# Perceiver block on one core: the last keys' probabilities copied to both partition halves, their values computed 512 queries wide amid the next scores, and the left key's scalings pinned in order

## The chip, the cores and the metric

The kernel runs on one core of one Trainium2 chip. The metric is device time in microseconds. A core has TensorE (PE) for matmuls, VectorE (DVE), ScalarE (ACT) and GpSimd (POOL) for the rest, and SyncE (SP), whose queue issues most of the transfers here; ACT's queue issues a few too. Each engine runs its own list of instructions in order and waits on semaphores for the others.

## The reference

Six sublayers follow each other, each added to `x` (8 batches of 64 tokens, width 512): cross attention, a block attention with a Fourier transform, a mixture of experts, a second cross attention, an attention with relative positions and a ternary feed-forward. The change touches the first sublayer alone:

```python
x = x + _L0_xattn_ref(_layernorm(x, axis=-1), ctx_1024, mask_BxS2_bf1,
                      L0_xattn_Wq, L0_xattn_Wkv, L0_xattn_Wout, L0_xattn_b_out)
```

It has 16 heads of width 64. For each batch and head the 64 queries are scored against 1601 keys that come from `ctx_1024` (8 x 1601 x 512), a softmax over the masked scores follows, the probabilities weigh the values, and a projection returns to width 512. All of it is float32.

## The kernel before

**Tiling.** The function `l0_xattn` holds this sublayer. The key weights are folded into the queries, so that scores are `ctx` times a 512-wide query (`qk`) and values are a 512-wide mixture of `ctx` rows (`a`), which the value weights turn afterwards (`v_ps`, line 699). A step takes one batch and half of the heads: 512 columns (4 head pairs g, 2 heads h of each, 64 queries q), so there are 16 steps. Even steps begin a new batch.

**Keys.** The 1601 keys are 12 blocks of 128 (`LAST`), 64 more (the *tail*), and one single *left* key. The 12 blocks are taken as 6 pairs. For each pair the product is formed with seven smaller products instead of eight (a Strassen-like scheme, class `Run`): `mul(..., n, ...)` is product n, and `p1`, `p5`, `u2`, `c11`, `c12`, `c22`, `c21` are its partial results and sums. Products 7 and 4 of one pair are issued within the next pair (`seventh`, `fourth`). In the scores, ACT copies `p1`, `p5` and `u2` out of PSUM and makes `c21`; DVE makes `c11`, `c12` and `c22`, and the running maximum `m` (lines 481, 484). Products 6, 7 and 4 add into the same PSUM tile `x_`, so 7 comes after `u2` has been copied from it and 4 after `c22` has read it. The four extra operands per key pair are made by `Quarters.left` on POOL, lines 138 to 141, 24 operations for a batch. In odd steps the finished key columns are read back from memory (`kept`), with no POOL work.

**Tail.** Its scores lie in `tail`: 256 columns, head h of each pair on partition half h. `attend_tail` (line 630) multiplies these probabilities with the tail's `ctx` rows, which lie on both halves: eight matmuls of 64 rows by 256 columns (line 641), whose results ACT copies into `a` (line 645). `attend` then adds the 12 blocks' values onto `a`.

**Left key.** Its score is a weighted sum over the 512 rows of `qk`: ACT scales the four row blocks (lines 492 and 497, tiles `by` and `by_c` of one tag with two buffers), POOL adds three times (line 498), and two matmuls against ones (`one_ps`, line 516) sum over partitions.

**Order.** A step of the loop at line 735 records: loads, `scores` of this step, `attend_tail` of the step before, `top_of` (transposes `m` with `m_ps`, reduces it and spreads it again with `top_ps`), `attend` of the step before, and `softmax` of this step. The text is not the order on the engines. A list scheduler, which works with modelled durations, orders each engine's instructions; `tc.keep_in_program_order` pins an instruction behind the one recorded last on its engine. Before the change only the writes to `kept` (line 205) are pinned in this stage.

**PSUM.** `ps_x`, `ps_y` and `ps_z` have two banks each for the products; `ps_m` has two for everything else (tag `mm`): tail scores, `one_ps`, `a_ps`, `m_ps`, `top_ps`, sums and side work. Side work of other parts (queries of the other batches, ternary weights) runs between, through `some` and `aside`.

Of the kernel before, what the change touches and what calls it, by code (L numbers as in the profile page):

```python
# [10 lines left out]
F32 = mybir.dt.float32  # L11
# [3 lines left out]
AF = mybir.ActivationFunctionType  # L15
# [5 lines left out]
P = 128  # L21
B, S, D = 8, 64, 512
NT = B * S // P
DC = D // P
# [3 lines left out]
NG = 8  # L28
# [87 lines left out]
H2 = P // 2  # L116
NK = len(KT)
TAIL, LAST = KT[-1][1], NK - 1
HALF = NG // 2 * P
QH = HALF // 2  # L120
NPAIR = LAST // 2
WIDE = LAST * HALF + 2 * QH
assert TAIL == H2 + 1


# [18 lines left out]
def l0_xattn(K, x, d, ternary, kept):  # L144
# [6 lines left out]
    tc, nc = K.tc, K.nc  # L151
    with ExitStack() as es:
# [19 lines left out]
        zp = es.enter_context(tc.tile_pool(name="a_z", bufs=1))  # L172

        def parts_of(wide):
            at = LAST * HALF
            return wide[:, :at].rearrange("p (k n) -> p k n", n=HALF), wide[:, ds(at, QH)], wide[:, at + QH :]

        def of_heads(t, h):
            return t.rearrange("p (g h q) -> p g h q", h=2, q=S)[:, :, h, :]
# [142 lines left out]
        norm_rest = K.normalizer(zp, x[:, 1:, :])  # L322
        load_weights(1)
        m8 = wp.tile([B * NK, P], U8, tag="m8", name="m8")
        m32 = tp.tile([P, QH], F32, tag="p1", name="m32")[: B * NK].rearrange("r (j n) -> r j n", j=2)
        nc.scalar.dma_start(m8, d["mask"])
        load_columns_tail(0)
        ctxT = load_columns(0)
# [76 lines left out]
        class Run:  # L405
# [6 lines left out]
            def add(self, mul, take):  # L412

                x_, y_, z_ = (
                    pool.tile([P, HALF], F32, tag=tag, name=f"{tag}_ps")[:, :QH]
                    for pool, tag in ((ps_x, "x"), (ps_y, "y"), (ps_z, "z"))
                )
                p1 = tp.tile([P, QH], F32, tag="p1", name="p1")
                u2 = tp.tile([P, QH], F32, tag="u2", name="u2")
                p5 = tp.tile([P, QH], F32, tag="p5", name="p5")  # L420
                mul(x_, 1, True)
                take.p1(p1, x_)
                self.seventh()
                mul(z_, 5, True)
                take.p5(p5, z_)
                mul(y_, 2, True)
                take.c11(y_, p1)
                self.fourth()
                mul(x_, 6, False)
                take.u2(u2, x_)  # L430
                mul(z_, 3, False)
                take.c12(z_, u2)
                self.before = mul, take, x_, p5
# [49 lines left out]
                    for k in (self.k, self.k + 1):  # L483
                        nc.vector.tensor_max(self.m, self.m, self.s[:, k, :])  # L484

        def scores(b, qkt, ctxT):
            qk, qt = qkt
            first = before is None
            wide = sp.tile([P, WIDE], F32, tag="s", name="s")
            s, tail, one = parts_of(wide)  # L490
            by = tp.tile([P, HALF], F32, tag="by", name="by")
            nc.scalar.activation(
                by, qk[:, 0, :], AF.Identity, bias=bias_left[:, b : b + 1], scale=left[:, 0, b : b + 1]
            )
            for c in range(1, DC):
                more = tp.tile([P, HALF], F32, tag="by", name="by_c")
                nc.scalar.activation(more, qk[:, c, :], AF.Copy, scale=left[:, c, b : b + 1])
                nc.gpsimd.tensor_add(by, by, more)
            m = tp.tile([P, HALF], F32, tag="m", name="m", bufs=1)
            right = {  # L500
                1: qk[:, 0:2, :QH], 2: qk[:, 2:4, :QH], 3: qk[:, 2:4, QH:],
                4: qt[:, 3], 5: qt[:, 0], 6: qt[:, 1], 7: qt[:, 2],
            }
            ps = ps_m.tile([P, HALF], F32, tag="mm", name="s_ps")[:, :QH]
            for c in range(DC):
                for h in range(2):
                    nc.tensor.matmul(
                        ps[ds(h * H2, H2)], lhsT=ctxT_tail[:, c, :], rhs=of_heads(qk[:, c, :], h),
                        start=c == 0, stop=c == DC - 1,
                    )  # L510
            nc.scalar.activation(tail, ps, AF.Identity, bias=bias_tail[:, b : b + 1], scale=1.0)

            def score_of_one():
                ps = ps_m.tile([P, HALF], F32, tag="mm", name="one_ps")[:, :QH]
                for h in range(2):
                    nc.tensor.matmul(ps[ds(h * H2, H2)], lhsT=ones, rhs=of_heads(by, h), start=True, stop=True)
                nc.scalar.copy(one, ps)

            if not first:
                score_of_one()  # L520
            run = Run()
            for i in range(NPAIR):

                def mul(ps, n, start, i=i):
                    for e in range(2):
                        nc.tensor.matmul(  # L526
                            ps,
                            lhsT=ctxT[i][:, Quarters.LEFT[n], ts(e, P)],
                            rhs=right[n][:, e, :],
                            start=start and e == 0,  # L530
                            stop=e == 1,
                            skip_group_check=not start,
                        )

                run.add(mul, Scores(s, m, b, i))
                some(2)
                next(aside, None)
                if first and i == NPAIR - 2:
                    score_of_one()
                if i == NPAIR - 1:  # L540
                    for h in range(2):
                        r = ds(h * H2, H2)
                        for rest in (tail, one):
                            m_h = of_heads(m[r], h)
                            nc.vector.tensor_max(m_h, m_h, rest[r].rearrange("p (g q) -> p g q", q=S))
            run.end()
            return wide, m

# [12 lines left out]
        def softmax(wide, top):  # L561

            parts = []
            s, tail, one = parts_of(wide)
            rest = wide[:, LAST * HALF :]
            for h in range(2):
                r = ds(h * H2, H2)
                rest_h = rest[r].rearrange("p (i g q) -> p i g q", i=2, q=S)
                nc.vector.tensor_sub(
                    rest_h, rest_h, of_heads(top[r], h).unsqueeze(1).to_broadcast([H2, 2, NG // 2, S])  # L570
                )
            nc.scalar.activation(rest, rest, AF.Exp)
            for k in range(0, LAST, 2):
                n = 2
                nc.vector.tensor_sub(s[:, k : k + n], s[:, k : k + n], top.unsqueeze(1).to_broadcast([P, n, HALF]))  # L575
# [14 lines left out]
            for h in range(2):  # L590
                r = ds(h * H2, H2)
                total_h = of_heads(total[r], h)
                nc.vector.tensor_add(total_h, total_h, tail[r].rearrange("p (g q) -> p g q", q=S))
            return parts, total, one

        class Mixed:
# [30 lines left out]
            def c21(self, ps):  # L627
                nc.vector.tensor_add(self.of(1, 0), ps, self.of(1, 0))

        def attend_tail(wide):  # L630

            a = tp.tile([P, DC, HALF], F32, tag="a", name="a", bufs=1)
            _, tail, _ = parts_of(wide)
            for c in range(0, DC, 2):
                heads = [
                    ps_m.tile([P, HALF], F32, tag="mm", name="a_ps").rearrange("p (i n) -> p i n", i=2) for _ in range(2)
                ]
                for i in range(2):
                    for h in range(2):
                        r = ds(h * H2, H2)  # L640
                        nc.tensor.matmul(
                            heads[h][:, i], lhsT=ctx_tail[r, ts(c + i, P)], rhs=tail[r], start=True, stop=True
                        )
                for h in range(2):
                    nc.scalar.copy(
                        a[:, c : c + 2].rearrange("p i (g h q) -> p i g h q", h=2, q=S)[:, :, :, h, :],
                        heads[h].rearrange("p i (g q) -> p i g q", q=S),
                    )
            return a

        def attend(b, half, soft, ctx, a, o, first):

# [31 lines left out]
            one = one.rearrange("p (g q) -> p g q", q=S)  # L684
            nc.vector.tensor_add(rs, sums, one)
            nc.vector.reciprocal(rs, rs)
            if b == 0:
# [47 lines left out]
        for step in range(2 * B + 1):  # L735
            if step < 2 * B:
                b, half = divmod(step, 2)
                if step:
                    now, ctxT = queries_of(b, half), load_columns(b, half)
                    if half == 0:  # L740
                        load_columns_tail(b)
                wide, m = scores(b, now, ctxT)
            if before:
                b0, half0 = divmod(step - 1, 2)
                a = attend_tail(before[0])
                if half0 and b0 + 1 < B:
                    load_rows_tail(b0 + 1)
            if step < 2 * B:
                top = top_of(m)
                if step == 1:  # L750
# [1757 lines left out]
```

## Time and profile before

| | us |
|---|---|
| median of three runs | 3070.31 (3068.79 to 3075.41) |
| profiled execution, its own time | 3067.53 |
| span of the profiled execution | 3065.8 |

The page gives busy times by engine, a picture of the span in 40 slices, the transfers, the chain of work that ended last, and the costliest groups. A group line names the kernel's line, engine and operation, out<-in, count, then busy us, mean ns, and the idle time before with what ended it. Some of the stage that the change touches:

```profile
L526 PE MATMUL x_ps<-qt,ctxT 128*128 128x256 f32 x1152 | 287.1, 383 | 12.6 <-DVE s L465 12.6
L665 PE MATMUL x_ps<-pt,ctx 128*128 128x256 f32 x1152 | 275.1, 381 | 0.6 <-DVE u L607 0.5
L138 POOL TENSOR_TENSOR ctx<-ctx 128x256 f32<-128x256 f32 x96 | 73.9, 770 | 605.9 <-DMA ctx<-in_ctx 461.3
```

Lines 526 and 665 are the products of the scores and of the values. Each float32 matmul leaves two records, so a product of the scores with its two matmuls shows as x4. Records of PE overlap their successors, so their durations add up to more than the time PE spends. The first sublayer takes about the first 1,525 us; the mean granted TensorE clock is 0.986.

A timeline line has the start and the duration of a run of equal instructions, engine, line and tiles, the count, and in brackets the idle time before it with what ended it. A line of the chain has start, duration, and what the time was spent in.

### The profile page before, as it was taken

Reading aid. Unit: us, or ns where it says so; the run is one execution under the profiler, and the core shown is the slowest. Engines: PE = TensorE matmul, PEld = TensorE weight load, DVE = VectorE, ACT = ScalarE, POOL = GpSimd, SP = SyncE. Lnnn points to the kernel's source line nnn. Section 1 sums busy time; section 2 is a strip of 40 time slices with the busy share of each in tenths; the row PEclk is TensorE's granted clock in tenths of the full one; section 3 lists DMA queues with packets and bytes.
Section 4 is the critical chain, followed back from the end, with each engine's and each line's share of the span. In section 5 each row is a group of like instructions: output and inputs, shape, how many; then the busy total and the mean of one; then the engine's idle time right before and its main releaser. Section 6 shows DMA issues by size and latency. Waiting matters only on the chain.

```text
span 3065.8 us, 41049 instructions
## 1 busy us (share of the span) xinstructions
PE 2965.6 (97%) x15650; PEld 2261.9 (74%) x15650; DVE 1917.8 (63%) x3383; ACT 878.3 (29%) x1636; POOL 924.6 (30%) x813
## 2 busy tenths in 40 slices
PE   8899999999999999999999999999999999999897
PEld 6777677787878887888745445788888888888764
DVE  4856455666667777666553243387677676676838
ACT  2422322233222232222021222333333323323224
POOL 3441342543625353442201001403404314224011
PEclk9999999999999999999999999999999999999989
DMA  9264364353655455352468986212021020120260
GB/s 320 79 223 160 115 219 173 118 190 136 219 194 190 165 180 187 107 191 101 162 216 313 345 283 203 73 33 77 5 89 52 28 89 29 51 91 10 101 86 14
DMA packets 288529, 430.52 MB, mean 140 GB/s; under 512 B 51126, under 2 KB 187326, under 8 KB 284110
## 3 DMA queue, kind: packets, MB, share of 16 engines
q1 hardware_dynamic: 273145, 389.59, 38.3%
q10 hardware_dynamic: 14549, 36.21, 3.3%
q8 instruction: 124, 2.03, 0.3%
q0 software_dynamic: 640, 2.10, 0.2%
q14 instruction: 71, 0.58, 0.1%
HBM read 352.80 MB, written 75.04 MB: 140 GB/s over the span
## 4 chain that ended last, share of the span: by engine, by line
PE 85%; DVE 6%; DMA 4%; POOL 2%; ACT 2%; issue 1%; SPq 0%; POOLq 0%; DVEq 0%; ACTq 0%
PE x_ps L1606 11%; PE x_ps L526 10%; PE x_ps L665 10%; PE y_ps L1606 8%; PE s_ps L1776 6%; PE z_ps L526 5%; PE z_ps L665 5%; PE oe_ps L1321 4%; PE h_ps L1294 4%; PE acc L1831 3%; PE y_ps L526 3%; PE y_ps L665 2%; DMA qk<-qk_all 2%; PE v_ps L699 1%; PE sum_ps L1653 1%
## 5 line engine op out<-in xcount | busy, mean ns | idle before, releaser
L1666 POOL TENSOR_TENSOR r<-r,minus_half 128x52 f32<-128x52 f32 x32 | 277.0, 8674 | 552.7 <-DVE r L1665 552.7
L526 PE MATMUL x_ps<-qt,ctxT 128*128 128x256 f32 x1152 | 287.1, 383 | 12.6 <-DVE s L465 12.6
L665 PE MATMUL x_ps<-pt,ctx 128*128 128x256 f32 x1152 | 275.1, 381 | 0.6 <-DVE u L607 0.5
L526 PEld LDWEIGHTS x_ps<-qt,ctxT 128*128 128x128 f32 x1152 | 216.5, 190 | 55.8 <-DVE s L465 20.8
L138 POOL TENSOR_TENSOR ctx<-ctx 128x256 f32<-128x256 f32 x96 | 73.9, 770 | 605.9 <-DMA ctx<-in_ctx 461.3
L665 PEld LDWEIGHTS x_ps<-pt,ctx 128*128 128x128 f32 x1152 | 216.9, 190 | 34.0 <-DVE a L622 1.6
L1776 PE MATMUL s_ps<-qb,kT 128*128 128x256 f32 x832 | 201.2, 382 | 0.0
L484 DVE TENSOR_TENSOR m<-m,s 128x512 f32<-128x512 f32 x160 | 131.0, 819 | 78.3 <-ACT s L479 76.2
L1776 PEld LDWEIGHTS s_ps<-qb,kT 128*128 128x128 f32 x832 | 155.0, 190 | 27.2 <-issue 4.9
L1786 DVE TENSOR_TENSOR s<-s_ps,r 128x512 f32<-128x512 f32 x192 | 126.7, 683 | 13.5 <-PE s_ps L1776 11.3
L465 DVE SCALAR_TENSOR_TENSOR s<-y_ps,bias,p 128x256 f32<-128x256 f32 x96 | 46.4, 483 | 131.7 <-PE y_ps L526 127.9
L1816 DVE TENSOR_TENSOR s<-s,top_ps 128x1792 f32<-128x1792 f32 x64 | 117.9, 1884 | 16.5 <-PE top_ps L1812 16.3
L1817 ACT ACTIVATE s<-s 128x1792 f32<-128x1792 f32 x64 | 101.1, 1591 | 66.2 <-DVE s L1816 66.2
L1831 PE MATMUL acc<-s,v 128*64 128x128 f32 x1664 | 115.9, 281 | 3.7 <-ACT s L1817 3.7
L1831 PEld LDWEIGHTS acc<-s,v 128*64 128x64 f32 x1664 | 98.4, 139 | 26.9 <-issue 22.6
L1294 PE MATMUL h_ps<-w,tok 128*128 128x512 f32 x256 | 117.3, 593 | 0.0
L575 DVE TENSOR_TENSOR s<-s,top_ps 128x1024 f32<-128x1024 f32 x96 | 115.9, 1210 | 0.4
L1321 PE MATMUL oe_ps<-w,hT 128*128 128x512 f32 x256 | 115.6, 593 | 0.0
L589 DVE TENSOR_TENSOR total<-total,s 128x512 f32<-128x512 f32 x160 | 112.5, 703 | 4.4 <-ACT s L576 0.9
L1313 ACT ACTIVATE hT<-hT_ps,L0f_be,L0f_g 128x128 f32<-128x128 f32 x128 | 55.5, 456 | 179.7 <-PE hT_ps L1312 116.9
L526 PE MATMUL x_ps<-qk,ctxT 128*128 128x256 f32 x384 | 103.8, 390 | 1.0 <-ACT s L479 1.0
L1606 PE MATMUL y_ps<-ctxT,L1x_WkT 128*128 128x256 f32 x384 | 102.2, 381 | 0.0
(476 smaller groups left out, 6351.3 us busy)
## 6 DMA issues: line engine op xcount, KB each, us to landing
w<-in_L0f_W SPq DMA_DIRECT2D x64, 1024.0 KB, 7.1
ctx<-in_ctx SPq DMA_DIRECT2D x192, 256.0 KB, 3.9
kept<-ctxT SPq DMA_DIRECT2D x48, 896.0 KB, 8.0
ctxT<-kept SPq DMA_DIRECT2D x48, 896.0 KB, 4.7
ctxT<-kept SPq DMA_DIRECT2D x24, 1792.0 KB, 7.2
ctxT<-in_ctxT SPq DMA_DIRECT2D x96, 256.0 KB, 4.4
wvT<-in_L0x_WvT SPq DMA_DIRECT2D x16, 1024.0 KB, 9.1
qk<-qk_all SPq DMA_DIRECT2D x15, 1024.0 KB, 6.4
```

Source lines behind the costliest of these rows:

```text
L484: nc.vector.tensor_max(self.m, self.m, self.s[:, k, :])
L526: nc.tensor.matmul(ps, lhsT=ctxT[i][:, Quarters.LEFT[n], ts(e, P)], rhs=right[n][:, e, :], start=start and e == 0, stop=e == 1, skip_group ...
L575: nc.vector.tensor_sub(s[:, k : k + n], s[:, k : k + n], top.unsqueeze(1).to_broadcast([P, n, HALF]))
L665: nc.tensor.matmul(ps, lhsT=ctx[pair][:, Quarters.LEFT[n], ts(m, P)], rhs=right[n][:, i, :], start=start and i == 0, stop=i == 2, skip_gro ...
L1294: nc.tensor.matmul(ps, lhsT=self.tok[:, c, :], rhs=self.w1[n][:, c, :], start=c == 0, stop=c == DC - 1)
L1321: nc.tensor.matmul(ps, lhsT=self.hT[:, f, :], rhs=self.w2[f // 4][:, f % 4, :], start=f == 0, stop=f == 15)
L1606: nc.tensor.matmul(ps, lhsT=left(n, e), rhs=right(n, e), start=start and e == 0, stop=e == 1, skip_group_check=not start,)
L1666: nc.gpsimd.tensor_tensor(r, r, minus_half, ALU.pow)
L1776: nc.tensor.matmul(ps[:, i].rearrange("p h q -> p (h q)"), lhsT=kT[c][:, ts(k0 + i, P)], rhs=qb[c].rearrange("p h q -> p (h q)"), start=Tr ...
L1786: nc.vector.tensor_mul(out, ps, by)
L1816: nc.vector.tensor_sub(part, part, top.to_broadcast([P, n, 2 * P]))
L1831: nc.tensor.matmul(acc[ds(64 * j, 64), c, :], lhsT=v[:, k, ds(c * P + 64 * j, 64)], rhs=s[:, k, ts(j, P)], start=k == 0, stop=k == NK - 1,)
```

## The change

The diff makes four edits to `l0_xattn`.

1. The tail's probabilities get a 512-wide place, like a key block. Each half computes its own heads' columns as before. After the exponential, two transfers on ACT's queue copy each half's columns to the other half, so that both halves hold all 512. They are pinned.
2. `attend_tail` is called for one pair of row blocks at a time, with two matmuls of 64 rows by 512 columns, one on each half, and two copies of 512 columns. The calls (`within`) stand within the next step's scores, after its third and fifth pair, no longer after the scores.
3. The maxima with `tail` and `one` stand at the third pair in all steps but the first, no longer at the last. The subtraction of the maximum and the exponential on `tail` and `one` are split into four and three instructions instead of two and one.
4. The left key's scalings on ACT and additions on POOL are pinned in program order, in all steps but the first. `p1` and `u2` keep one buffer each instead of two, as the wider place takes 1 KB more per partition in each of two buffers.

```diff
-WIDE = LAST * HALF + 2 * QH
+WIDE = (LAST + 1) * HALF + QH
...
-                p1 = tp.tile([P, QH], F32, tag="p1", name="p1")
-                u2 = tp.tile([P, QH], F32, tag="u2", name="u2")
+                p1 = tp.tile([P, QH], F32, tag="p1", name="p1", bufs=1)
+                u2 = tp.tile([P, QH], F32, tag="u2", name="u2", bufs=1)
...
-            nc.scalar.activation(
+            pinned = tc.keep_in_program_order if before else lambda ins: ins
+            pinned(nc.scalar.activation(
                 by, qk[:, 0, :], AF.Identity, bias=bias_left[:, b : b + 1], scale=left[:, 0, b : b + 1]
-            )
+            ))
...
-                nc.scalar.activation(more, qk[:, c, :], AF.Copy, scale=left[:, c, b : b + 1])
-                nc.gpsimd.tensor_add(by, by, more)
+                pinned(nc.scalar.activation(more, qk[:, c, :], AF.Copy, scale=left[:, c, b : b + 1]))
+                pinned(nc.gpsimd.tensor_add(by, by, more))
...
-                if i == NPAIR - 1:
+                if i == (NPAIR - 1 if first else 2):
                     for h in range(2):
                         r = ds(h * H2, H2)
-                        for rest in (tail, one):
+                        for rest in (of_heads(tail[r], h), one[r]):
...
+                if i in (2, 4):
+                    within(i - 2)
...
-            nc.scalar.activation(rest, rest, AF.Exp)
+            for h in range(2):
+                r = ds(h * H2, H2)
+                rest = of_heads(tail[r], h)
+                nc.scalar.activation(rest, rest, AF.Exp)
+            for h in range(2):
+                to = ds((1 - h) * H2, H2)
+                tc.keep_in_program_order(nc.scalar.dma_start(of_heads(tail[to], h), of_heads(tail[ds(h * H2, H2)], h)))
+            nc.scalar.activation(one, one, AF.Exp)
...
-        def attend_tail(wide):
-
-            a = tp.tile([P, DC, HALF], F32, tag="a", name="a", bufs=1)
+        def attend_tail(wide, a, c):
+
             _, tail, _ = parts_of(wide)
...
+            pair = [ps_m.tile([P, HALF], F32, tag="mm", name="a_ps") for _ in range(2)]
+            for h in range(2):
+                r = ds(h * H2, H2)
+                nc.tensor.matmul(pair[h], lhsT=ctx_tail[r, ts(c + h, P)], rhs=tail[r], start=True, stop=True)
+            for h in range(2):
+                nc.scalar.copy(a[:, c + h, :], pair[h])
...
+            def within(c):
+                if before:
+                    attend_tail(before[0], a, c)
+
+            if step < 2 * B:
+                wide, m = scores(b, now, ctxT, within)
+            else:
+                for c in (0, 2):
+                    within(c)
```

More of the change, by code (lines that the diff above doesn't have):

```diff
@@ L174, in parts_of @@
         def parts_of(wide):
-            at = LAST * HALF
-            return wide[:, :at].rearrange("p (k n) -> p k n", n=HALF), wide[:, ds(at, QH)], wide[:, at + QH :]
+            s = wide[:, : NK * HALF].rearrange("p (k n) -> p k n", n=HALF)
+            return s[:, :LAST], s[:, LAST], wide[:, NK * HALF :].rearrange("p (g q) -> p g q", q=S)
         def of_heads(t, h):
@@ L324, in l0_xattn @@
         m8 = wp.tile([B * NK, P], U8, tag="m8", name="m8")
-        m32 = tp.tile([P, QH], F32, tag="p1", name="m32")[: B * NK].rearrange("r (j n) -> r j n", j=2)
+        m32 = tp.tile([P, QH], F32, tag="p1", name="m32", bufs=1)[: B * NK].rearrange("r (j n) -> r j n", j=2)
         nc.scalar.dma_start(m8, d["mask"])
@@ L484, in c21, with scores @@
                         nc.vector.tensor_max(self.m, self.m, self.s[:, k, :])
-        def scores(b, qkt, ctxT):
+        def scores(b, qkt, ctxT, within):
             qk, qt = qkt
@@ L510, in scores @@
                     )
-            nc.scalar.activation(tail, ps, AF.Identity, bias=bias_tail[:, b : b + 1], scale=1.0)
+            for h in range(2):
+                r = ds(h * H2, H2)
+                nc.scalar.activation(
+                    of_heads(tail[r], h), ps[r].rearrange("p (g q) -> p g q", q=S), AF.Identity,
+                    bias=bias_tail[r, b : b + 1], scale=1.0,
+                )
             def score_of_one():
@@ L516, in score_of_one @@
                     nc.tensor.matmul(ps[ds(h * H2, H2)], lhsT=ones, rhs=of_heads(by, h), start=True, stop=True)
-                nc.scalar.copy(one, ps)
+                nc.scalar.copy(one, ps.rearrange("p (g q) -> p g q", q=S))
             if not first:
@@ L539, in scores @@
                     score_of_one()
-                if i == NPAIR - 1:
+                if i == (NPAIR - 1 if first else 2):
                     for h in range(2):
                         r = ds(h * H2, H2)
-                        for rest in (tail, one):
+                        for rest in (of_heads(tail[r], h), one[r]):
                             m_h = of_heads(m[r], h)
-                            nc.vector.tensor_max(m_h, m_h, rest[r].rearrange("p (g q) -> p g q", q=S))
+                            nc.vector.tensor_max(m_h, m_h, rest)
+                if i in (2, 4):
+                    within(i - 2)
             run.end()
@@ L564, in softmax @@
             s, tail, one = parts_of(wide)
-            rest = wide[:, LAST * HALF :]
             for h in range(2):
                 r = ds(h * H2, H2)
[L568 to L571, printed above, removed]
-            nc.scalar.activation(rest, rest, AF.Exp)
+                for rest in (of_heads(tail[r], h), one[r]):
+                    nc.vector.tensor_sub(rest, rest, of_heads(top[r], h))
+            for h in range(2):
[6 more added lines that the diff above has]
+            nc.scalar.activation(one, one, AF.Exp)
             for k in range(0, LAST, 2):
@@ L592, in softmax @@
                 total_h = of_heads(total[r], h)
-                nc.vector.tensor_add(total_h, total_h, tail[r].rearrange("p (g q) -> p g q", q=S))
+                nc.vector.tensor_add(total_h, total_h, of_heads(tail[r], h))
             return parts, total, one
@@ L628, in c21 @@
                 nc.vector.tensor_add(self.of(1, 0), ps, self.of(1, 0))
-        def attend_tail(wide):
-            a = tp.tile([P, DC, HALF], F32, tag="a", name="a", bufs=1)
+        def attend_tail(wide, a, c):
             _, tail, _ = parts_of(wide)
[L634 to L649, printed above, removed]
+            pair = [ps_m.tile([P, HALF], F32, tag="mm", name="a_ps") for _ in range(2)]
+            for h in range(2):
+                r = ds(h * H2, H2)
+                nc.tensor.matmul(pair[h], lhsT=ctx_tail[r, ts(c + h, P)], rhs=tail[r], start=True, stop=True)
+            for h in range(2):
+                nc.scalar.copy(a[:, c + h, :], pair[h])
         def attend(b, half, soft, ctx, a, o, first):
@@ L683, in attend @@
             rs = tp.tile([P, NG // 2, S], F32, tag="rs", name="rs", bufs=1)
-            one = one.rearrange("p (g q) -> p g q", q=S)
             nc.vector.tensor_add(rs, sums, one)
@@ L741, in l0_xattn @@
                         load_columns_tail(b)
-                wide, m = scores(b, now, ctxT)
             if before:
                 b0, half0 = divmod(step - 1, 2)
-                a = attend_tail(before[0])
-                if half0 and b0 + 1 < B:
-                    load_rows_tail(b0 + 1)
+                a = tp.tile([P, DC, HALF], F32, tag="a", name="a", bufs=1)
+            def within(c):
[6 more added lines that the diff above has]
+                    within(c)
+            if before and half0 and b0 + 1 < B:
+                load_rows_tail(b0 + 1)
             if step < 2 * B:
```

## The prediction

> **What bounds the kernel.** I read the page first (busy shares, chain that ended last), then the stage the diff touches, which is the first 1,520 us: 16 overlapping steps of scores, softmax and values.
>
> ```profile
> PE 2965.6 (97%) x15650; PEld 2261.9 (74%) x15650; DVE 1917.8 (63%) x3383; ACT 878.3 (29%) x1636; POOL 924.6 (30%) x813
> PE 85%; DVE 6%; DMA 4%; POOL 2%; ACT 2%; issue 1%; SPq 0%; POOLq 0%; DVEq 0%; ACTq 0%
> ```
> TensorE (PE) sets the end. So an edit counts only through PE: work taken from it, or time in which it stands. The busy column hides part of that: a record of 256 columns lasts 0.38 us but the next starts 0.216 us later, so I count starts. Each float32 matmul is two records; a product of the scores (two matmuls) costs 0.86 us, one of the values (three) 1.30.
>
> Next, the chain in order of time, at the end of one step's scores (step 6):
>
> ```profile
> 643.47 9.01 DMA qk<-qk_all
> ...
> 652.56 0.81 ACT by L492
> 653.37 0.48 ACT a L645
> ...
> 653.90 1.11 PE top_ps L558 x4
> ```
> The chain leaves PE. `top_ps` waits for a bank that a copy of the last keys' values (line 645) frees; that copy stands on ScalarE (ACT) behind the next step's `by` (line 492), and `by` waits for the next queries' transfer. Over the stage `top_ps` waits 15.8 us so.
>
> **The step boundary, where the gain lies.** Timeline of PE in a step without that stall (14):
>
> ```profile
> 1345.67 1.13 PE L641 MATMUL a_ps<-s,ctx_tail 64*128 64x256 f32 x6
> 1347.16 1.13 PE L526 MATMUL x_ps<-qt,ctxT 128*128 128x256 f32 x4 [0.36 <-DVE s L465]
> 1348.22 1.13 PE L641 MATMUL a_ps<-s,ctx_tail 64*128 64x256 f32 x6
> 1349.59 1.13 PE L641 MATMUL a_ps<-s,ctx_tail 64*128 64x256 f32 x4 [0.24 <-ACT a L645]
> 1350.65 0.66 PE L553 MATMUL m_ps<-ident,m 128*128 128x128 f32 x4
> ```
> From the sixth pair's `y_ps` product to the first values product after `top_ps`, less 0.216 us per score or value record and 0.108 per transposition, steps 4 to 15 spend 8.9, 8.9, 8.1, 7.0, 5.3, 5.3, 5.9, 4.7, 6.1, 4.5, 4.5, 4.5: 73.6 us. Steps 2 and 3, less their side work, 11.2 and 10.1.
>
> Afterwards each step has two visits of two matmuls, 512 wide, one on each partition half. The nearest row has 64 rows by 384:
>
> ```profile
> 161.05 0.92 PE L271 MATMUL qk_ps<-qT,w 64*128 64x384 f32 x4
> 161.89 0.70 PE L665 MATMUL x_ps<-s,ctx 128*128 128x256 f32 x2
> ```
> Two matmuls in 0.84 us, of which 0.65 is two records of 384 columns: the halves ran side by side, and 0.19 is entering and leaving. At 512: 2 x 0.43 + 0.19 = 1.05; two visits 2.1 us.
>
> Here a rule differs from the row. The Trainium skill (TensorEngine Tiling, Key Properties) says that different tiles execute loads and matmuls in parallel. By that alone the eight matmuls of before would already take 4 x 0.43 = 1.7 us, and pairing would be worth nothing. The rows above span 3.9 us outside the scores product: the built order puts matmuls of the same half next to each other, and only some overlap. I take the row; by the rule the sum would lose 1.8 us x 14 = 25.
>
> What is late next at the boundary? The four maxima with `tail` and `one` (0.42 us each on VectorE) leave it. In the built order of the changed kernel (it holds no times), the fourth product of the last pair stands behind three values matmuls, `m_ps` behind three more, `top_ps` behind two, and `top_ps` waits for VectorE alone. By the rows (0.48 for a sum, 0.69 a maximum, 0.47 the ACT pass) I count 0.45 us of standing: 0.2 at `m_ps`, 0.1 at `top_ps`, the rest hand-over. Step 1 of before already had this order but with the maxima in it and stood 2.1; that is the upper end. Steps 4 to 15: 73.6 - 12 x 2.55 = 43.0, less 1.7 where a weight pass on ACT stands before the last `c21` (steps 8, 11) = 41.3. Steps 2 and 3, with side work fighting for the same two banks: 21.3 - 2 x 4.1 = 13. The last tail saves 1.5; step 1 loses 0.5. **Gain 55.3.**
>
> **The pins, where the loss lies.** Pinned behind what was recorded before them on their engine, the three POOL additions to `by` now follow, in every even step from 2 on, all 24 `Quarters.left` operations of the batch's key columns. Before, they ran some 30 us ahead. Timeline around the start S of the scores of step 8, and one addition:
>
> ```profile
> 750.58 1.28 POOL L498 TENSOR_TENSOR by<-by,by_c 128x512 f32<-128x512 f32 x1 [0.83 <-ACT by_c L497]
> ...
> 783.74 0.87 POOL L138 TENSOR_TENSOR ctxT<-ctxT 128x256 f32<-128x256 f32 x1 [5.41 <-PE v_ps L699]
> 784.41 1.13 PE L526 MATMUL x_ps<-qk,ctxT 128*128 128x256 f32 x4
> ...
> 792.94 0.73 POOL L141 TENSOR_TENSOR ctxT<-ctxT 128x256 f32<-128x256 f32 x1
> ```
> The last `left` ends at S + 9.3 (steps 6, 8, 10, 14: 9.2 to 9.3; 12: 10.0), because the last three pairs' slots come free only when the values end. The additions then end at S + 10.6, 12.7 and 14.9 (1.28 each, 0.83 for the scaling between). In the built order ACT has: p1, p5, second `by_c`, u2, third `by_c`. The second `by_c` needs the first addition, so u2 of the first pair ends at 9.3 + 1.28 + 0.1 + 0.72 + 0.4 = S + 11.8. Behind it waits PE: product 7 accumulates into the bank u2 is copied from. PE would be there at 6 x 0.864 = 5.2, so it stands 6.7 us; then `one_ps` waits for the third addition. It comes 14 matmuls after S in steps 10, 12, 14 (stands 8.9, 9.6, 8.9 in all) and 16 in steps 6, 8 (8.05 each). Step 2, with the last `left` at S + 11.8: 8.4. Step 4, where pinned `by` follows the side work's copies instead: about 2. **Loss 53.9.** Before shows that ACT can be held this way, harmlessly:
>
> ```profile
> 840.20 0.72 ACT L497 ACTIVATE by_c<-qk,left 128x512 f32<-128x512 f32 x1 [7.48 <-POOL by L498]
> 840.83 1.04 ACT L576 ACTIVATE s<-s 128x1024 f32<-128x1024 f32 x1
> ```
> The exponentials started 11 us after `top_ps` and PE did not stand: the values they feed come a step later. That also covers the edits I cost at nothing:
> - **The two copies between halves** (64 KB each, 256-byte pieces). The nearest row, `ctx_tail` of 128 KB, lands in 3.7 us; the skill (DMA: Bandwidth & Descriptors, Specifications) speaks against pieces under 512 B, with a read-modify-write. Doubled, 7.4 us; the reader is some 60 us away. Their issue may hold ACT until an earlier transfer lands (0 to 5 us), inside the slack above. SP's queue gets nothing new. Without the cover, 5 x 16 = 80.
> - **Four subtractions and two exponentials instead of two and one**: +0.4 us VectorE a step, VectorE 63% busy. Bounds 0 to 6 in all.
> - **p1 and u2 with one buffer**: p1 of the next pair waits for c11, done some 3 us before. 0 to 5 in all.
> - **The values' copies now amid the scores**: two of 0.58 us stand on ACT before the next pair's p1, which PE needs three products (2.6 us) later. The next `ctx_tail` load on SP waits for the second visit, one pair before the row load behind it does: nothing, at most 1 a step.
> - **Exponentials no longer behind `by_c`**: earlier, worth nothing now.
> - Everything after the stage stands in the same order on every engine.
>
> **Sum.** -55.3 + 53.9 = -1.4. The profiled execution took 3067.5 (span 3065.8 and 1.7 around it): 3066.1. Its like among the three runs is their median, 3070.3: **3069**.
>
> **Rivals.**
> - *Shorter stall.* If the last `left` ends one group (2.9 us) nearer S, since the idle VectorE no longer slows them (one took 1.89 instead of 0.73): 6 x 2.9 = 17 less, 3052. For: that 1.89. Against: the other groups ran at full pace already.
> - *No stall* (the pins do not do what they say, ACT not held at u2): 3069 - 54 = 3015. Against: the built order, and the 7.48 above.
> - *Slower: the boundary stays occupied.* If `m_ps` and the fourth product stand 2.1 as in step 1 rather than 0.45, 14 x 1.65 = 23: 3092. It decides as soon as VectorE reaches c22 more than 2.2 us after product 7 starts. For: VectorE also serves the values' first sums there. Against: the maxima that delayed it are gone. With the last `left` also 1 us late, 3098.
> - *Slower: the halves do not overlap at 512*: 16 x 2 x 0.86 = 28: 3097. Against: the 384 row.
>
> **Chances.** About 0.2% (6 us) is what a measurement tells from no change. Forecast 0.43, own range 3058 to 3080 (the sum of two terms near 55, each known to some 5): 0.29 within 6 us, 0.06 faster, 0.08 slower. Shorter stall 0.18, no stall 0.05: faster. Occupied boundary 0.24, no overlap 0.10: slower. Faster 0.29, same 0.29, slower 0.42. The range drops no stall, the far half of no overlap and some of the edges: 3047 to 3092.
>
> **What would show it.** Right: no `top_ps` wait on ACT; a visit of four 512-wide records in about 1.05 us; in even steps PE standing 6 to 7 us before a product on ACT's u2, then 1 to 2 at `one_ps` on POOL, and `by` additions ending near S + 15. Wrong: those additions done by S + 6, or stalls in odd steps, or standing at `m_ps` above 1 us.

## The result, and the profile after

| | us |
|---|---|
| after, median of four runs | 3101.11 (3095.06 to 3101.91) |
| before, four runs on the same chip | 3069.55 (3067.62 to 3075.41) |
| ratio, with its 95% interval | 1.0095 (1.0077 to 1.0114) |
| span of the profiled execution, before and after | 3065.8 and 3093.2 |

The kernel became about 29 us slower; 3069 had been forecast, in a range up to 3092. The busy shares of the page:

```profile
PE 2960.6 (96%) x15522; PEld 2237.9 (72%) x15522; DVE 1933.7 (63%) x3415; ACT 900.7 (29%) x1684; POOL 937.5 (30%) x813
```

They say what they said before: TensorE still bounds. The waits of TensorE over the stage say more. Columns: us in total, times, longest. First one line of before, then the changed kernel:

```profile
PE top_ps L558 <- ACT a L645: 15.8, 6, 4.0
```

```profile
PE x_ps L532 <- ACT u L460: 35.6, 6, 6.4
PE one_ps L522 <- POOL by L499: 17.0, 6, 9.3
PE m_ps L561 <- DVE m L484: 6.5, 12, 1.4
PE x_ps L666 <- DVE u L619: 2.9, 6, 0.9
```

`top_ps` no longer waits for ACT, and in its place come the two waits that were forecast: the product on u2, and `one_ps` on the pinned additions. (The longest wait at `one_ps`, 9.3 us, is in step 1 and was not forecast.) PE at the start of the scores of step 14:

```profile
1334.11 1.03 PE L532 MATMUL x_ps<-qk,ctxT 128*128 128x256 f32 x4
1341.36 2.07 PE L532 MATMUL x_ps<-qt,ctxT 128*128 128x256 f32 x4 [6.22 <-ACT u L460]
1344.54 1.12 PE L522 MATMUL one_ps<-by,ones 128*64 128x256 f32 x4 [1.10 <-POOL by L499]
1345.59 2.08 PE L532 MATMUL z_ps<-qt,ctxT 128*128 128x256 f32 x4
```

The stand of 6.2 us was expected; the second column was not. Four records take 2.07 us instead of 1.03. The windows show why (stretch, length, busy us of PE, PEld, DVE, ACT, POOL with instructions in brackets; then granted clock, DMA share, GB/s):

```profile
1341.40:1344.50 3.10, 2.03 (x4) 1.13 (x4) 0.91 (x2) 0.98 (x2) 2.25 (x2) 0.50 1.00 421
1344.50:1349.20 4.70, 4.66 (x13) 3.20 (x14) 0.00 (x0) 0.74 (x2) 0.00 (x0) 0.50 0.16 66
```

After the stand the granted clock is 0.50 over these 7.8 us, and 0.77 over the 3.4 us that follow: half the clock for some 9 us. The boundary, on the other hand, looks as forecast (step 15):

```profile
1466.01 1.46 PE L666 MATMUL z_ps<-pt,ctx 128*128 128x256 f32 x6
1467.74 0.66 PE L561 MATMUL m_ps<-ident,m 128*128 128x128 f32 x4 [0.27 <-DVE m L484]
1468.23 1.03 PE L666 MATMUL y_ps<-s,ctx 128*128 128x256 f32 x4
1469.18 0.65 PE L566 MATMUL top_ps<-ident,top 128*128 128x128 f32 x4
```

It stands 0.3 us at `m_ps` and not at `top_ps`. By the prediction's count of the boundary, 8.1 us are left over steps 4 to 15, 0.67 a step, where before had 73.6. The copies between halves, reckoned at 7.4 us each, landed 2.1 to 2.3 us after their issue.

So both forecast mechanisms are there. The question for the runs is why their sum came out some 30 us worse. In two profiles I measured each step from one `top_ps` to the next, before and after: +9.8 us in step 1, then +2.9, -3.0, +0.5, -6.5, +2.6, -4.5, +3.1, 0.0, +7.8, -0.9, +9.4, +0.6, +11.2, -0.2 in steps 2 to 15: 32.8 in all; the next sublayer's first matmul comes 31.0 later (1558.3 instead of 1527.3).

### The profile page after: what moved, and what is told of

It reads as the page before. It is cut to its first block, busy times and chain, and to the rows that moved or that the text cites. A ratio compares the mean times of both kernels' runs of the same rounds, so it can differ in the third digit from the quotient of the medians.

```text
span 3093.2 us, 40814 instructions
## 1 busy us (share of the span) xinstructions
PE 2960.6 (96%) x15522; PEld 2237.9 (72%) x15522; DVE 1933.7 (63%) x3415; ACT 900.7 (29%) x1684; POOL 937.5 (30%) x813
## 4 chain that ended last, share of the span: by engine, by line
PE 50%; DVE 4%; DMA 1%; ACT 1%; issue 1%; POOL 0%; SPq 0%; POOLq 0%; DVEq 0%; ACTq 0%
PE x_ps L1615 11%; PE y_ps L1615 8%; PE s_ps L1785 6%; PE oe_ps L1330 4%; PE h_ps L1303 4%; PE acc L1840 3%; PE x_ps L666 2%; PE x_ps L532 1%; PE sum_ps L1662 1%; PE z_ps L666 1%; PE z_ps L532 1%; PE out_ps L1858 1%; PE hT_ps L1321 1%; PE xf_ps L1247 1%; PE k_ps L2127 0%
## 5 line engine op out<-in xcount | busy, mean ns | idle before, releaser
L532 PE MATMUL x_ps<-qt,ctxT 128*128 128x256 f32 x1152 | 296.4, 392 | 40.5 <-ACT u L460 35.6
L532 PEld LDWEIGHTS x_ps<-qt,ctxT 128*128 128x128 f32 x1152 | 223.5, 196 | 85.1 <-ACT u L460 38.0
L484 DVE TENSOR_TENSOR m<-m,s 128x512 f32<-128x512 f32 x160 | 123.0, 769 | 77.2 <-ACT s L479 74.5
L601 DVE TENSOR_TENSOR total<-total,s 128x512 f32<-128x512 f32 x160 | 134.8, 842 | 3.9
L588 ACT ACTIVATE s<-s 128x1024 f32<-128x1024 f32 x96 | 100.9, 1056 | 37.0 <-DVE s L587 34.9
L465 DVE SCALAR_TENSOR_TENSOR s<-z_ps,bias,u 128x256 f32<-128x256 f32 x96 | 46.4, 483 | 98.8 <-ACT u L460 50.5
```

The costliest lines, as they stand in the source:

```text
L532: nc.tensor.matmul(ps, lhsT=ctxT[i][:, Quarters.LEFT[n], ts(e, P)], rhs=right[n][:, e, :], start=start and e == 0, stop=e == 1, skip_group ...
L601: nc.vector.tensor_add(total, total if k > 1 else s[:, 0, :], s[:, k, :])
```

## Experiments

Ratios are to the kernel before on the same chip, with 95% intervals. Step times compare two profiles.

**The pins.** The changed kernel without them, with them in odd steps alone, and the kernel before with them alone:

```diff
-            pinned = tc.keep_in_program_order if before else lambda ins: ins
+            pinned = lambda ins: ins
```

> The changed kernel without the pins on the left key's scalings and additions; the pins on the two copies between halves stay. Theory (the pins cost all of the loss, by standing and by the slow records after it): the waits of the first pair on u2 and of one_ps on the additions go, in steps 1, 2, 4, 6, 8, 10, 12 and 14, with the slow records behind them; from the excess of each step in the changed kernel over its neighbours that is 9.5 + 8.4 + 2.5 + 8 + 8.3 + 11 + 11 + 11.5 = 70 us, so 3101 - 70 = about 3031. Rival (the loss lies in the rest of the change: copies between halves, single buffers, split exponentials): 3085 to 3101.

Measured: 3034.9, ratio 0.9876 (0.9848 to 0.9903). The theory held.

```diff
-            pinned = tc.keep_in_program_order if before else lambda ins: ins
+            pinned = tc.keep_in_program_order if before and step % 2 and step > 1 else lambda ins: ins
```

> The changed kernel with the pins in odd steps from 3 on only. Theory: the pins cost only in even steps (behind the key columns' additions on POOL) and in step 1 (behind the exponentials on ACT); so as without any pin, about 3031, within 6 us of it. Rival (the pins cost in odd steps too): halfway, about 3060.

Measured: 0.9899 (0.9868 to 0.9930), 7 us above the kernel without pins, where the theory had allowed 6. The intervals overlap, so the times alone don't tell whether pins in odd steps cost something. By steps the odd ones from 3 on took 9.9 us more than without pins, the even ones 0.6 less.

```diff
-                nc.scalar.activation(more, qk[:, c, :], AF.Copy, scale=left[:, c, b : b + 1])
-                nc.gpsimd.tensor_add(by, by, more)
+                pinned(nc.scalar.activation(more, qk[:, c, :], AF.Copy, scale=left[:, c, b : b + 1]))
+                pinned(nc.gpsimd.tensor_add(by, by, more))
```

(and the first scaling, `by`, likewise)

> The kernel before with the pins alone. Theory: the same stands and slow records arise without the rest of the change, some 70 us, less a part of the 15.8 us that top_ps waits behind by on ScalarE: 3070 + 70 - 10 = about 3130. Rival (the stall needs the new order of the tail's values and maxima): within 15 us of 3070.

Measured: 1.0124 (1.0100 to 1.0149), 38 us, where some 60 had been expected. The same two waits stand in its trace, 34.2 us on u2 and 17.2 at `one_ps`; the stall needs nothing else of the change. The pins cost less here than the 67 us between the ratios 1.0095 and 0.9876, partly because the pins also remove the 15.8 us for which `top_ps` waited behind `by`.

So the pins cost about 67 us and the rest of the change gains 38. The profiles, step by step, split both sums:

| us | forecast | measured | from |
|---|---|---|---|
| pins, even steps from 2 on | 53.9 | 55.5 | after against no pins: 9.2, 2.5, 6.5, 7.2, 8.5, 9.4, 12.2 |
| pins, step 1 | 0 | 4.2 | the same |
| pins, odd steps from 3 on | 0 | 8.1 | the same: 2.4, 0.0, 0.6, 1.5, 0.7, 1.9, 1.0 |
| gain, steps 4 to 15 | 41.3 | 28.6 | no pins against before |
| gain, steps 2 and 3 | 13 | 11.8 | the same |
| gain, step 1 | -0.5 | -5.7 | the same |
| gain, the last tail | 1.5 | 2.2 | the same, from step 15 on |

**Which pin.** The pins on POOL's additions alone, then those on ACT's scalings alone:

```diff
-            pinned(nc.scalar.activation(
+            (nc.scalar.activation(
...
-                pinned(nc.scalar.activation(more, qk[:, c, :], AF.Copy, scale=left[:, c, b : b + 1]))
+                (nc.scalar.activation(more, qk[:, c, :], AF.Copy, scale=left[:, c, b : b + 1]))
```

> The changed kernel with the pins on POOL's additions alone; ScalarE's scalings are left to the scheduler. Theory (POOL's additions behind the 24 operations of the key columns are the cause in even steps, ScalarE's pins in step 1 alone): even steps as in the changed kernel, step 1 some 4 us better; ratio to before about 1.008, 1.005 to 1.010. Rival (it is ScalarE's pinned scalings that hold u2): near the kernel without pins, 0.988 to 0.992.

Measured: 1.0082 (1.0063 to 1.0102), as the theory had it. ACT's pins are not needed for the stall: 35.0 us on u2 stay, since the scheduler too puts a scaling before u2. But step 1 became 3.6 us shorter than in the changed kernel, and the odd steps from 3 on 7.9 us, about what the pins cost there. Steps 2 and 4, with their side work, took 10.5 us more in this profile.

```diff
-                pinned(nc.gpsimd.tensor_add(by, by, more))
+                (nc.gpsimd.tensor_add(by, by, more))
```

> The changed kernel with the pins on ScalarE's scalings alone; POOL's additions are left to the scheduler, which puts them ahead of the key columns' operations. Theory: even steps don't stall; only step 1 stays worse, by some 4 us: ratio to before about 0.989, 3039 us. Rival (ScalarE's pins hold u2): 1.005 to 1.010.

Measured: 0.9951 (0.9933 to 0.9968). The stall of the even steps is gone, apart from 2.1 us in step 4, but the kernel is some 23 us slower than without pins, where 4 were expected. Neither theory had this. By steps, 4.6 us lie in step 1, 3.7 in step 4 and 7.3 in the odd steps from 3 on; most of what lies outside step 1 is spread over the values of the steps:

```profile
PE x_ps L666 <- DVE u L619: 10.5, 9, 2.6
```

With two more such lines (4.7 us on line 640, 3.9 on line 637) TensorE waits 19.1 us for VectorE in the values. It is 6.7 in the changed kernel, 8.0 in that without pins, 0.5 before.

**Is VectorE the next bound?** Without the pins, and with four of VectorE's eleven additions of the sum (128x512) left out:

```diff
-            for k in range(1, LAST):
+            for k in range(1, LAST - 4):
```

> The changed kernel without the pins, and the sum of the probabilities leaves out the last four of the twelve key blocks: four additions of 128x512 fewer on VectorE in each step, 3 us of its work amid the values. Theory (with the boundary emptied VectorE has become the next bound in the values: TensorE waits 8 us there for its partial results, in the kernel before 0.5): these waits go, 8 to 12 us less than without pins alone, ratio to before 0.984 to 0.985. Rival (these waits come from the order of the values' products, or count nothing): 0.9876 as without pins.

Measured: 0.9835 (0.9818 to 0.9851), 12 us less than without pins. The waits of the values for VectorE fell from 8.0 to 1.1 us. Without pins most of them stood in this line:

```profile
PE x_ps L666 <- DVE u L619: 5.5, 5, 1.6
```

The same omission in the kernel before was not tried; its values wait for VectorE for 0.5 us in all. One wait, in the values after step 11's `top_ps` in the kernel without pins, shows how tight it is. First VectorE, whose lines have no idle time, then PE:

```profile
1091.50 1.48 DVE L605 TENSOR_TENSOR total<-total,s 64x256 f32<-64x256 f32 x2
1093.01 0.42 DVE L640 TENSOR_TENSOR a<-x_ps,a 128x256 f32<-128x256 f32 x1
1093.35 0.41 DVE L619 TENSOR_TENSOR u<-x_ps,a 128x256 f32<-128x256 f32 x1
```

```profile
1093.82 1.56 PE L666 MATMUL x_ps<-pt,ctx 128*128 128x256 f32 x6 [1.44 <-DVE u L619]
```

The product waits for u (line 619); that stands behind two additions of the sum. In the whole span VectorE is busy 63% of the time. In the values of one step it is another matter; before, then without pins:

```profile
1353.00:1390.00 37.00, 37.00 (x188) 31.80 (x187) 31.34 (x56) 7.65 (x9) 9.95 (x10) 1.00 0.22 78
```

```profile
1319.50:1357.00 37.50, 37.50 (x237) 32.07 (x235) 34.20 (x60) 9.67 (x13) 11.52 (x11) 1.00 0.31 112
```

VectorE's is the third busy time: 31.3 of 37.0 us, 85%, then 34.2 of 37.5, 91%. Both stretches begin just after step 14's `top_ps`.

**Why ACT's pins make it tighter.** VectorE's additions of the sum got longer, though they are the same instructions. Each of these lines is from another kernel: before, without pins, and with ACT's pins alone (steps 6 to 15):

```profile
L589 DVE TENSOR_TENSOR total<-total,s 128x512 f32<-128x512 f32 x91 | 63.5, 697 | 3.0 <-ACT s L576 0.9
```

```profile
L601 DVE TENSOR_TENSOR total<-total,s 128x512 f32<-128x512 f32 x100 | 75.6, 756 | 4.1 <-ACT s L588 1.5
```

```profile
L601 DVE TENSOR_TENSOR total<-total,s 128x512 f32<-128x512 f32 x97 | 89.7, 925 | 2.4
```

One takes 0.70 us, 0.76, and 0.93. The pinned scalings come after the exponentials, and so POOL's three additions come then too, 4 to 8 us later against the next scores than without pins (steps 8 to 15), amid VectorE's sums. The Trainium skill (SBUF — State Buffer, Who interferes with whom) has a rule for such pairs: a VectorE instruction with two SBUF inputs contends with a GpSimd instruction that reads SBUF. The trace agrees, pair by pair. With ACT's pins alone the sums that have no POOL instruction beside them take 0.68 us, as before and without pins; 50 overlap one of these three additions (11 without pins, 2 before): the 25 of them that start first take 0.68 too, the 25 that start amid an addition 1.47 on average. One addition and the two sums beside it:

```profile
1359.76 0.67 DVE L601 TENSOR_TENSOR total<-total,s 128x512 f32<-128x512 f32 x1
1359.78 1.78 POOL L499 TENSOR_TENSOR by<-by,by_c 128x512 f32<-128x512 f32 x1 [0.83 <-ACT by_c L498]
1360.69 1.42 DVE L601 TENSOR_TENSOR total<-total,s 128x512 f32<-128x512 f32 x1
```

POOL's addition is drawn out as well, to 1.78 us from the 1.28 of before. To test what this costs, ACT's pins stay and the three additions go:

```diff
                 pinned(nc.scalar.activation(more, qk[:, c, :], AF.Copy, scale=left[:, c, b : b + 1]))
-                (nc.gpsimd.tensor_add(by, by, more))
```

> The kernel with the pins on ScalarE's scalings alone, which took 0.9951 of the kernel before instead of 0.9876, and POOL's three additions left out in every step: the left key's score keeps only its first of four row blocks. Theory (the pinned scalings move POOL's additions into the stretch in which VectorE sums the probabilities; VectorE's sums took 0.93 us there on average instead of 0.76, and TensorE waits for VectorE in the values): without the additions the waits for VectorE fall to those of the kernel without pins or below, ratio 0.984 to 0.989. Rival (the place of the scalings on ScalarE itself, behind the exponentials, costs): 0.993 to 0.996.

Measured: 0.9825 (0.9786 to 0.9864). The loss is gone: what costs is POOL at work beside VectorE's sums, which now take 0.73 us each:

```profile
L600 DVE TENSOR_TENSOR total<-total,s 128x512 f32<-128x512 f32 x100 | 72.7, 727 | 2.5
```

The values wait 2.6 us for VectorE, instead of 19.1. To leave out the additions without any pin was not tried, so a small cost of the scalings' own place may be hidden in this gain.

**The pins at another place.** The scalings and additions recorded right after the queries' loads and still pinned:

```diff
-                    now, ctxT = queries_of(b, half), load_columns(b, half)
+                    now = queries_of(b, half)
+                    bys.append(by_of(b, now[0]))
+                    ctxT = load_columns(b, half)
```

> The changed kernel with its pins, but the left key's scalings and additions are recorded right after the queries' loads, ahead of the key columns' 24 operations. Theory (not the pin but what it is pinned behind costs): no stall in even steps; the additions still fall into VectorE's sums as with ScalarE's pins alone: ratio to before 0.989 to 0.996. Rival (the additions, which wait for the queries' transfer, now hold the 24 operations behind them and the key columns come late): above 1.0.

Measured: 0.9940 (0.9924 to 0.9956), as with ACT's pins alone, with the same waits for VectorE (18.7 us), and no stall from step 6 on. What stalls the even steps is not that the additions are pinned but what they are pinned behind.

**The slow records after the stand.** Useless matmuls fill the stand, once 12 before the waiting product, then 14 there and 5 before `one_ps`, which is pinned behind them:

```diff
+                    if fill:
+                        spare = ps_m.tile([P, HALF], F32, tag="mm", name="spare_ps")[:, :QH]
+                        for e in range(FILL):
+                            keep(nc.tensor.matmul(
+                                spare, lhsT=ctxT[0][:, Quarters.LEFT[1], ts(e % 2, P)], rhs=right[1][:, e % 2, :],
+                                start=e == 0, stop=e == FILL - 1,
+                            ))
```

> The changed kernel with 12 more matmuls of 128x256 in each even step from 2 on, into a spare bank that nobody reads, just ahead of the product that waits for u2 (5.2 us of work in a stand of 6 to 7 us); one_ps is kept behind that product, as it was. Theory (TensorE's clock drops because it stood, and the slow records after the stand are a cost of their own): POOL's additions end no sooner, but the records after them run at full pace, 2.3 to 4.1 us less in each of steps 2, 6, 8, 10, 12 and 14: 3101 - 18 = about 3083, although 28 to 36 us of work are added. Rival (the slow records come from something else, such as the transfers that load TensorE's operands at that time, or the standing alone costs): 3101, or later.

Measured: 1.0119 (1.0090 to 1.0149). From step 6 on the stand before the product shrank to 0.7 to 0.9 us, but TensorE then stood 2.05 to 2.35 us before `one_ps`, and records at half speed followed that (granted clock 0.50 for 6.2 us in step 14).

> As with the 12 further matmuls, which did not make it faster: there the wait for u2 shrank to 0.9 us, but TensorE then stood 2.1 to 2.7 us before one_ps, and 1.8 to 3.4 us of slow records followed that. Now 14 matmuls stand before the product that waits for u2 and 5 more before one_ps, so that TensorE hardly stands at all. Clock theory: the slow records in even steps vanish, about 2.7 x 6 = 16 us less than the changed kernel, which stood at 1.0095 of the kernel before: ratio about 1.004. Rival (slow records have another cause, or the clock doesn't matter): ratio 1.009 to 1.012.

Measured: 1.0127 (1.0110 to 1.0144). The slow records are gone in the even steps from 6 on, as step 14 shows, yet the kernel is no faster:

```profile
1344.27 6.21 PE L538 MATMUL spare_ps<-qk,ctxT 128*128 128x256 f32 x28
1350.52 1.13 PE L543 MATMUL x_ps<-qt,ctxT 128*128 128x256 f32 x4
1351.49 2.32 PE L553 MATMUL spare_ps<-qk,ctxT 128*128 128x256 f32 x10
1353.74 0.65 PE L524 MATMUL one_ps<-by,ones 128*64 128x256 f32 x4
```

By steps against the changed kernel: -2.3 and -3.1 us in steps 12 and 14, but +0.8 to +1.0 in steps 6, 8 and 10, and +4.6 and +5.3 in steps 2 and 4, where the 8.5 us of added work are longer than the stand. In steps 6 and 8 `one_ps` was also moved ahead by two products.

The changed kernel's own trace gives the price of the clock more directly. Slow records before `one_ps` cost hardly anything, as `one_ps` would else wait for the third addition. Those behind it come to 2.0, 2.1 and 2.7 us over full pace in steps 10, 12 and 14, to 0.8 in step 2 and to 0.1 in steps 6 and 8, where two more products precede `one_ps`. So the clock has a price of its own, but it is no large part of the 29 us. As a forecast of the whole time the theory failed.

**The parts of the gain.** Without pins, the maxima with `tail` and `one` back at the last pair, and the tail's values back behind the scores:

```diff
-                if i == (NPAIR - 1 if first else 2):
+                if i == NPAIR - 1:
```

> The changed kernel without the pins, with the maxima of tail and left key back at the last pair. Theory (the maxima delayed the boundary as they did in step 1 of the kernel before, 2.1 us instead of 0.5): 1.6 us in each of some 14 steps, ratio to before 0.9876 + 0.0075 = 0.995. Rival (VectorE has room at the boundary as well as at the third pair, where the four maxima now stand): 0.987 to 0.990.

Measured: 0.9872 (0.9832 to 0.9912). Moving the maxima bought nothing that can be measured. It did empty the boundary: by the count that gave 73.6 us before, 14.2 are left with the maxima at the last pair and 6.4 at the third. Yet steps 4 to 15 together differ by only 2.7 us. A gain counted at the boundary is not a gain of the step.

```diff
-                if i in (2, 4):
-                    within(i - 2)
...
+            for c in (0, 2):
+                within(c)
```

> The changed kernel without the pins, with both visits to the tail's values recorded after the scores, as in the kernel before, still 512 wide. Theory (moving them amid the scores is what empties the boundary; at the boundary two visits share two banks with m_ps and top_ps, and each waits for copies of 1.07 us): 2 us in each of 15 steps, ratio 0.9876 + 0.010 = 0.997. Rival (the width alone gives the gain, the place nothing): 0.987 to 0.990.

Measured: 1.0014 (1.0001 to 1.0027). The gain hangs on the place of the tail's values. Still 512 wide but back at the boundary, they bring back the wait for ACT's copies, and more of it than before (24.4 us instead of 15.8):

```profile
PE top_ps L564 <- ACT a L648: 24.4, 9, 4.4
```

That the narrow matmuls of before, amid the scores, would gain as much was not tried.

The fastest kernel that leaves nothing out is thus the change without its pins, with the maxima at either place: 0.987 to 0.988 of before.

## Why the prediction was wrong

**Right: the stall of the even steps, its sum in part by luck.** The additions behind the 24 operations, u2 behind a scaling, PE 6.1 to 6.5 us before the product from step 6 on, 1.1 to 1.4 at `one_ps` in steps 10 to 14, the additions' end near S + 15: all are in the trace. At `one_ps` PE is late by 8.1, 8.1, 8.8, 8.7 and 8.6 us in steps 6 to 14, where 8.05, 8.05, 8.9, 9.6 and 8.9 were forecast. That 53.9 stands against 55.5 hides two misses that largely cancel. The text left out that TensorE restarts at half its clock: the 6.8 us behind `one_ps` in steps 10, 12 and 14. The Trainium skill (TensorE: Matmul & The Clock Gate, What's actually happening) has the rule, that an idle window of about 3.4 us puts the clock back to half; here shorter stands were enough, as the run with 12 useless matmuls shows. The trace of before already had slow records after the `top_ps` waits, worth 1.0 to 2.3 us each, and I did not price them. Against that, the values ahead of steps 6 to 12 wait 0.9 to 1.5 us less for VectorE than without pins, since POOL's additions no longer lie amid them.

**Right: the boundary itself.** Its rest was 8.1 us after (6.4 without pins), 0.67 a step against 0.45. The halves overlap: a visit of four 512-wide records took 1.06 us against 1.05.

**Wrong: the gain of 55.3 us.** The step that failed is "What is late next at the boundary?", with its term of 41.3 us for steps 4 to 15, and the line that priced VectorE's work at nothing: "+0.4 us VectorE a step, VectorE 63% busy" (which also counts two exponentials where there are three). The count was made at the boundary and taken over to the step. The steps gained 28.6, and the trace has the difference of 12.7 in two terms.

First, in these steps the values wait for VectorE for 8.0 us, where before they waited 0.5. VectorE's subtractions cannot start before `top_ps`. In the kernel before, `top_ps` had only four records of the values ahead of it in most steps, as in step 14:

```profile
1351.14 1.03 PE L665 MATMUL x_ps<-s,ctx 128*128 128x256 f32 x4
1352.18 0.62 PE L558 MATMUL top_ps<-ident,top 128*128 128x128 f32 x4
```

With the boundary emptied, 16 stand ahead of it (ten of them in the lines of step 15 above). So behind `top_ps` TensorE has 12 x 0.216 = 2.6 us less of values to do, while VectorE has the same work. The 63% was an average over stages: in the values it was 85% already. When VectorE was relieved of four additions, 11 us came back in these steps.

Second, the hand-over around a visit was left out: the product before it takes 0.96 us and the one after it 0.97 instead of 0.86. So a visit costs 1.26 us, not 1.05, and 24 of them 5.0 us more.

**Wrong: no price for the pins in odd steps and step 1.** The text looked at the pinned additions for what stands behind them, and found nothing in odd steps; it did not ask what runs beside them. There they cost 8.1 us, and 4.2 in step 1; by the runs with one kind of pin these are ACT's. In step 1 the pinned scalings stand behind the exponentials: the first starts at 90.3 us, where it started at 76.7 before, and so `one_ps` waits 9.3 us for the additions. With ACT's pins alone the exponentials come earlier and the additions later, which cost 23 us, and without the additions none of it.

Step 1 lost 5.7 us even without pins, where 0.5 was forecast. There TensorE waits 3.3 us for ACT's p and 3.8 for VectorE; what sets that order was not tried, though relieving VectorE gave 4.0 us of it back, and the maxima at the last pair 4.8.

**The rivals.** None of the named ones came true: the boundary did not stay occupied, the halves do overlap, the stall was neither shorter nor absent. The time of the third (3092, 3098) was near by accident.

## What to carry to other kernels

Before an emptied stall is booked as gain, look at what will move into its place, and how busy the other engines are in that stage and not in the page's averages: here VectorE was at 85% there, and part of the gain was already spent. An instruction pinned in program order is late by all that its engine has been given before it, and it also moves in time against the engines that it disturbs; ask both. To undo one edit at a time and compare step by step showed here that one edit (the tail's values amid the scores) made all of the gain, and one (the pins) all of the loss.

## What the runs showed of the hardware

- After standing 6.2 us TensorE was granted 0.50 of its clock for some 9 us. Two stands of 0.7 to 0.9 and 2.05 to 2.35 us, with one product between them, were enough for half the clock too.
- The same addition of 128x512 on VectorE took 0.68 us with no POOL instruction beside it and beside one of POOL's additions of the same size 0.68 if it started first and 1.47 on average if POOL did. Its mean over ten steps was 0.70, 0.76 or 0.93 us, depending on when POOL's additions ran.
- Two matmuls of 64 rows by 512 columns, one on each partition half, took 1.06 us together, and 1.26 with what the products around them lost.
